# First cross-attention of a Perceiver stack: another order for the preparation of the keys

## Chip, cores and metric

The kernel runs on one core of one Trainium2 chip. The metric is the device time of one execution in microseconds (us). Before the change it was 652.71 us, the median of 3 runs (652.16 to 653.26). The core has five engines that run on their own and meet through semaphores: PE (TensorE: matmuls and, ahead of them, weight loads), DVE (VectorE), ACT (ScalarE), POOL (GpSimd) and SP (SyncE, which issues most of the DMAs). Each works through its own instructions in order.

## The reference

Twelve layers work one after the other on a latent array x of 2 batches by 64 rows by 256: four rounds of a cross-attention to a context (2 by 1024 rows by 192), a mixing layer and a mixture of experts. Only the first cross-attention is touched by the change:

```python
xn = layernorm(context)            # 2 x 1024 x 192
ln = layernorm(layernorm(x))       # 2 x 64 x 256
q = ln @ Wq.T
kv = concat([xn @ Wkv.T, ln @ Wlkv.T])       # 1024 context keys and 64 latent keys
q, k, v = split_heads(...)         # 4 heads of 64
qn, kn = rmsnorm(q) * qn_g / 8, rmsnorm(k) * kn_g
attn = softmax(where(mask, qn @ kn.T, -max)) # the latent keys are never masked
x = x + (attn @ v) @ Wo.T + bo
```

## The kernel before

The whole stack is one program. The first attention is the stage `l0x` (from L1148), about 9 to 78 us of the span. All 2 x 64 latent rows lie on the 128 partitions.

**Keys.** The context keys are made in four groups of 512, each one batch and two of its four key tiles in both halves; groups 0 and 1 are the first batch, 2 and 3 the second. A fifth group, LAT, is the latents' own keys and queries. For a group g these helpers are called, each of which emits instructions for one or two engines:

- `statistics(g)` (L1230): eight small DVE operations for mean and variance of four row tiles; `roots(g)` (L1238): the square root on ACT and its inverse on DVE; `normalise_rows(g)` (L1311): four POOL operations that normalise the context rows for use as values.
- `project(g)` (L1241): 16 matmul instructions into a pair of PSUM banks; `take(g)` (L1256): four DVE operations that scale the result by the inverse root and add a bias, into `kq`.
- `squares(g)` (L1265): one ACT operation; `sums(g)` (L1271): a DVE reduction and a square root on ACT; `over_rms(g)` (L1279): two small DVE operations and a large one that scales the keys.
- `turn_keys(g)` (L1288): for each half of the features four transposes on PE into one PSUM bank, and an ACT copy from it to `kT`. For LAT there are two transposes and three ACT copies for each half.

**Attention.** There are four query blocks a, b, c, d (batch and pair of heads). `scores(k)` (L1337) writes the scores of the context keys to a bank pair and those of the latent keys to a single bank, `extra`. `softmax(k)` (L1351) masks both with a custom DVE operation that also gives the minimum, and then takes the exponentials on ACT. `divisor`, `turn_p` (nine transposes into three single banks, emptied by DVE, ACT, DVE), `value_weights`, `weigh`, `turn_u` and `heads_of` follow. `hide_keys` (L1186) makes the mask on POOL.

**Fills.** `kv1.values_apart(b, t)` (L475) computes values of a later layer (`l1x`) in between. It is a generator: its first step takes two single banks and emits eight matmuls (half of the work), the second step the other eight, and the last two ACT copies that empty the banks. `steps(fill, 1)` runs one step, `steps(fill)` the rest. Another generator of the next stage, `kv1.keys` (L446, L451), is started right behind this stage with three steps.

**What sets the order.** The stage lies in `in_written_order()` (L295), which chains the instructions of PE, DVE, ACT and POOL each in the order in which the code emits them. So the code's order is the order on each engine, and an instruction that waits holds up all behind it on its engine. The three steps of `kv1.keys` lie outside and are placed by the framework's planner. PSUM is split into two pairs of banks and four single banks (`psum(2, 4)`); a bank is given to the next tile when the last reader of the old one is through. SBUF tiles rotate in the same way: `kq` and `p` (squares, then probabilities) have two buffers each.

The loop over the groups (L1452 to L1480) emits for g = 0 to 3: take and squares of the next group, over_rms of this one, the first half of a fill, turn_keys of this one (for g = 0 also LAT's and the fourth projection), sums of the next group, for g < 2 statistics, roots and row normalisation of group g + 2, then scores (a at g = 1, b at g = 2), at g = 2 also the table for the exponentials and the softmax of a, and the rest of the fill.

Of the kernel before, what the change touches and what calls it, by code (L numbers as in the profile page):

```python
# [12 lines left out]
AF = mybir.ActivationFunctionType  # L13
# [45 lines left out]
def tile_perceiver(ctx: ExitStack, tc: tile.TileContext, i: dict, out: bass.AP):  # L59
    nc = tc.nc  # L60
# [40 lines left out]
    def stat(n=1, name="stat"):  # L101
        return small.tile([P, n], F32, tag=f"s{n}", bufs=12 if n == 1 else 4, name=name)
# [130 lines left out]
    def table_for(func, behind):  # L233

        nc.scalar.activation(junk, behind, func, scale=0.0)  # L235

    def rstd_of(var, n=1, then=None, bias=eps, scale=1.0):

        root, r = stat(n, "root"), stat(n, "rstd")
        nc.scalar.activation(root, var, AF.Sqrt, bias=bias, scale=scale)  # L240
        if then is not None:
            table_for(then, root[:, 0:1])
        nc.vector.reciprocal(r, root)  # L243
        return r
# [288 lines left out]
    def steps(work, n=9):  # L533

        for _, _ in zip(range(n), work):
            pass
# [610 lines left out]
    with psum(2, 4), stage_pool(name="l0x", bufs=1) as pool, stage_pool(  # L1147
# [38 lines left out]
        def hide_keys():  # L1186
            nc.gpsimd.tensor_scalar(hide, m8, -1.0, BIG, ALU.add, ALU.mult)
# [42 lines left out]
        def statistics(g):  # L1230
            b, t = groups[g]
            mv[g] = small.tile([P, 4, 2], F32, tag="cx_mv", name="cx_mv")
            for k in range(4):
                st = stat(6, "bn_st")
                nc.vector.bn_stats(st, xh[:, b, k // 2, t + k % 2, :CD])
                nc.vector.bn_aggr(mv[g][:, k, :], st)

        def roots(g):  # L1238
            rstd[g] = rstd_of(mv[g][:, :, 1], 4)

        def project(g):  # L1241
            if g == LAT:
                kq[g] = prep.tile([P, 2, D], F32, tag="kql", bufs=1, name="kql")
                ps = bank()
                accumulate(ps, [(latT[:, c, :], wlkv[:, c, :]) for c in range(2)])
                return ps
            kq[g] = prep.tile([P, 4, D], F32, tag="kq", name="kq")
            ps = two_banks()
            context_values(ps, wkc, *groups[g])
            return ps  # L1250
# [6 lines left out]
        def take(g, ps):  # L1257
            for k in range(4):
                nc.vector.scalar_tensor_tensor(
                    kq[g][:, k, :], ps[:, k * D : (k + 1) * D], rstd[g][:, k : k + 1], bwk,  # L1260
                    ALU.mult, ALU.add,
                )
# [3 lines left out]
        def squares(g):  # L1266
            n = 2 if g == LAT else 4
            sq[g] = prep.tile([P, 4, D], F32, tag="p", name="sq")
            nc.scalar.activation(sq[g][:, :n], kq[g][:, :n], AF.Square)

        def sums(g):  # L1271
            n = 2 if g == LAT else 4
            rn[g] = stat(16, "rn")[:, : 4 * n]
            nc.vector.tensor_reduce(
                rn[g], sq[g][:, :n].rearrange("p t (h d) -> p (t h) d", h=4), AX.X, ALU.add
            )
            nc.scalar.activation(rn[g], rn[g], AF.Sqrt)

        def over_rms(g):  # L1279
            n = 2 if g == LAT else 4  # L1280
            nc.vector.tensor_scalar(rn[g], rn[g], 0.125, 1e-8, ALU.mult, ALU.max)
            nc.vector.reciprocal(rn[g], rn[g])
            by_head = kq[g][:, :n].rearrange("p t (h d) -> p (t h) d", h=4)
            nc.vector.tensor_tensor(
                by_head, by_head, rn[g].unsqueeze(2).to_broadcast([P, 4 * n, 64]), ALU.mult
            )

        def turn_keys(g):  # L1288
            n = 2 if g == LAT else 4
            for c in range(2):  # L1290
                ps = bank()
                for k in range(n):
                    nc.tensor.transpose(
                        ps[:, k * P : (k + 1) * P], kq[g][:, k, c * P : (c + 1) * P], ident
                    )
                if g == LAT:
                    nc.scalar.activation(kTl[:, c, :], ps[:, :P], AF.Copy, scale=col("l0x_kg"))
                    for h in range(2):
                        r = half[h]
                        nc.scalar.activation(  # L1300
                            qx[r, c, :, r],
                            ps[r, P : 2 * P].rearrange("p (b q) -> p b q", b=NB),
                            AF.Copy, scale=gq[r],
                        )
                else:
                    b, t = groups[g]
                    nc.scalar.activation(
                        kT[:, c, b, :, t : t + 2, :],
                        ps.rearrange("p (n t k) -> p n t k", n=2, t=2),
                        AF.Copy, scale=col("l0x_kg"),  # L1310
                    )  # L1311

        def normalise_rows(g):
            b, t = groups[g]
            for k in range(4):
                one = xh[:, b, k // 2, t + k % 2, :CD]
                nc.gpsimd.tensor_scalar(  # L1317
                    one, one, mv[g][:, k, 0:1], rstd[g][:, k : k + 1],
                    ALU.subtract, ALU.mult,
                )  # L1320
# [17 lines left out]
        def scores(k):  # L1338
            b, j = k
            q = qx[:, j, b, :]  # L1340
            sc[k], extra = two_banks(), bank()
            dst = [sc[k][:, n * 512 : (n + 1) * 512] for n in range(2)]
            for n in range(2):
                nc.tensor.matmul(
                    dst[n], q, kT[:, j, b, n].rearrange("p t k -> p (t k)"),
                    start=True, stop=True,
                )
            nc.tensor.matmul(extra[:, :P], q, kTl[:, j, :], start=True, stop=True)
            sc[k] = sc[k], extra

        def softmax(k):  # L1351

            main, extra = sc[k]
            b, _ = k
            neg, total = stat(2, "neg"), stat(2, "tot")
            p[k] = prep.tile([P, NK + P], F32, tag="p", name="p")
            for n, (keys, src, hidden_) in enumerate((
                (slice(NK, NK + P), extra[:, :P], hide_l[:, b, :]),
                (slice(0, NK), main, hide[:, b, :]),
            )):  # L1360
                nc.vector.tensor_tensor_reduce(
                    p[k][:, keys], src, hidden_, -1.0, NEG, ALU.add, ALU.min, neg[:, n : n + 1]
                )
            nc.vector.tensor_tensor(neg[:, 0:1], neg[:, 0:1], neg[:, 1:2], ALU.min)
            for n, keys in enumerate((slice(0, NK), slice(NK, NK + P))):
                nc.scalar.activation(
                    p[k][:, keys], p[k][:, keys], AF.Exp, bias=neg[:, 0:1], scale=-1.0,
                    accum_out=total[:, n : n + 1],
                )
            rinv[k] = total  # L1370
# [8 lines left out]
        def turn_p(k):  # L1379
            pT[k] = transposed(p[k], 9, prep, "pT", "pT")  # L1380
# [52 lines left out]
        psk = [project(0)]  # L1433
        statistics(0)
        roots(0)
        statistics(1)
        key_bias()
        psq = project_queries()
        roots(1)
        nc.scalar.copy(kq[LAT][:, 1, :], psq[:, :D])  # L1440
        take(0, psk[0])
        squares(LAT)
# [6 lines left out]
        normalise_rows(1)  # L1449
        psk.append(project(2))  # L1450
        a, b, c, d = ((b, j) for b in range(NB) for j in range(2))
        for g in range(4):  # L1452


            if g < 3:
                take(g + 1, psk[g + 1])
                squares(g + 1)
            over_rms(g)
            if g < 3:
                fill = kv1.values_apart(g // 2, 2 * (g % 2))  # L1460
                steps(fill, 1)
            turn_keys(g)
            if g == 0:
                turn_keys(LAT)
                psk.append(project(3))
            if g < 3:
                sums(g + 1)
            if g < 2:
                statistics(g + 2)
                roots(g + 2)  # L1470
                normalise_rows(g + 2)
            if g == 0:
                hide_keys()
            if g == 1:
                scores(a)
            if g == 2:
                scores(b)
                table_for(AF.Exp, rn[3][:, 0:1])
                softmax(a)
            if g < 3:  # L1480
                steps(fill)
        divisor(a)
        turn_p(a)
        softmax(b)
        value_weights()
        weigh(a)
# [1 line left out]
        divisor(b)  # L1488
        turn_p(b)
        turn_u(a)  # L1490
        softmax(c)
        weigh(b)
        scores(d)
# [1 line left out]
        divisor(c)  # L1495
        turn_p(c)
        turn_u(b)
        softmax(d)
        weigh(c)
        heads_of(b)  # L1500
# [1351 lines left out]
```

## Time and profile before

| what | value |
|---|---|
| median of the runs | 652.71 us |
| the profiled execution | 652.64 us |
| its span | 650.7 us |
| mean granted PE clock | 0.991 |
| first attention, statistics to its result | about 10.9 to 78.2 us |
| first scores (a) on PE | 35.01 us |
| first exponentials (a) on ACT | 45.83 us |
| value weights on PE | 50.11 us |
| result x of the stage on DVE | 77.81 us |

A row of the timeline gives the start in us from the span's start, the time that the instructions of one group took, the engine, the line, the operation, the tile written and the tiles read, the shapes and how many. Square brackets give how long the engine had been idle before it, and what ended the idle time. Matmuls are pipelined, so the time of several is less than the sum of their durations. A table by stretch gives for each engine the busy time and the number of instructions, and then the granted PE clock, the busy share of the DMA engines and GB/s.

### The profile page before, as it was taken

The page shows a single profiled execution, that of the slowest core. Times are in us where ns is not written, and L with a number is a line of the kernel's source. Part 1 is how long each engine was busy: PE and PEld are TensorE (multiplying, and loading weights), DVE is VectorE, ACT ScalarE, POOL GpSimd, SP SyncE. Part 2 cuts the span into 40 slices and gives each one's busy share as a digit, 9 for nine tenths or more (in the row PEclk, how much of TensorE's full clock was granted, in tenths as well). Part 3 has the DMA queues.
Part 4 walks back from the last instruction along what each step waited for, and adds up shares of the span by engine and source line. Part 5 has one row for each costly group of instructions (what it writes and reads, how often), then busy time and mean ns, then how long its engine had stood idle before and what let it go on. Part 6 is the DMA issues. An engine that isn't in the chain of part 4 may idle for free. (4 is left out here: it accounts for less than half of the span.)

```text
span 650.7 us, 11687 instructions
## 1 busy us (share of the span) xinstructions
PE 615.7 (95%) x4722; PEld 451.5 (69%) x4722; DVE 306.9 (47%) x871; ACT 258.4 (40%) x507; POOL 52.3 (8%) x88
## 2 busy tenths in 40 slices
PE   7989999999999969999999999999999989989996
PEld 3547659766754538999998688999984446775434
DVE  5875451268672014545554426625425247747111
ACT  2464462378732232323232434504422159742111
POOL 3540000000100000000000040040000000100000
PEclk9999999999999979999999999999999999999999
DMA  8970025920438477000000500010147910094870
GB/s 286 399 301 1 17 74 169 318 95 2 165 121 352 151 211 248 1 1 2 1 2 0 195 1 1 1 62 6 65 156 286 393 74 3 2 372 153 346 311 11
DMA packets 19441, 87.05 MB, mean 134 GB/s; under 512 B 2080, under 2 KB 6704, under 8 KB 11088
## 3 DMA queue, kind: packets, MB, share of 16 engines
q1 hardware_dynamic: 19120, 86.09, 35.8%
q8 instruction: 49, 0.80, 0.5%
q14 instruction: 16, 0.13, 0.1%
q10 hardware_dynamic: 256, 0.03, 0.0%
HBM read 85.98 MB, written 0.13 MB: 132 GB/s over the span
## 5 line engine op out<-in xcount | busy, mean ns | idle before, releaser
L2079 PE MATMUL bank<-l2x_ctx,p 128*128 128x193 f32 x256 | 48.1, 327 | 0.0
L2079 PEld LDWEIGHTS bank<-l2x_ctx,p 128*128 128x128 f32 x256 | 40.8, 190 | 0.4
L1714 DVE CUSTOM_DVE_ANT_0 p<-two_banks,zero 128x1024 f32<-128x1024 f32 x32 | 38.6, 1216 | 5.2 <-PE two_banks L1704 5.0
L1722 ACT ACTIVATE p<-p,negmax 128x1024 f32<-128x1024 f32 x32 | 36.9, 1154 | 4.7 <-DVE negmax L1714 4.7
L2043 DVE TENSOR_REDUCE l2x_mx<-two_banks 128x128 f32<-128x1024 f32 x16 | 19.6, 1225 | 26.5 <-PE two_banks L2035 26.5
L2028 PE MATMUL two_banks<-l2x_qA,ctxA 128*128 128x128 f32 x256 | 31.9, 278 | 0.0
L2028 PEld LDWEIGHTS two_banks<-l2x_qA,ctxA 128*128 128x128 f32 x256 | 30.3, 192 | 1.1 <-issue 1.0
L776 DVE COPY m_hT<-bank 128x512 f32<-128x512 f32 x12 | 8.3, 691 | 42.5 <-PE bank L770 42.5
L331 PE MATMUL bank<-ctxA,ones 128*128 128x256 f32 x94 | 25.8, 391 | 1.3 <-ACTq L1132 1.0
L2065 DVE TENSOR_TENSOR p<-two_banks,l2x_shift 128x512 f32<-128x512 f32 x32 | 20.6, 686 | 13.2 <-ACT l2x_shift L2060 13.2
L750 ACT ACTIVATE m_g<-two_banks 128x512 f32<-128x512 f32 x12 | 7.2, 598 | 47.1 <-PE two_banks L727 31.8
L235 ACT ACT_TABLE_LOAD x20 | 25.7, 1283 | 0.3
L751 DVE TENSOR_TENSOR m_prod<-two_banks,m_g 128x512 f32<-128x512 f32 x12 | 8.3, 691 | 35.8 <-ACT m_g L750 35.8
L2072 ACT ACTIVATE p<-p 128x512 f32<-128x512 f32 x32 | 19.7, 632 | 12.2 <-DVE p L2065 12.2
L1729 PEld LDWEIGHTS two_banks<-ident,p 128*128 128x128 f32 x128 | 13.7, 141 | 11.0 <-ACT pT L1758 9.1
L331 PEld LDWEIGHTS bank<-ctxA,ones 128*128 128x128 f32 x94 | 15.9, 190 | 5.6 <-issue 2.2
L1704 PE MATMUL two_banks<-n_kT,n_qx 32*128 32x512 f32 x128 | 19.2, 640 | 0.0
L1729 PE MATMUL bank<-ident,p 128*128 128x128 f32 x128 | 18.5, 280 | 0.5
L2035 PE MATMUL two_banks<-l2x_qB,ctxB 64*128 64x128 f32 x256 | 18.6, 285 | 0.0
L1317 POOL TENSOR_SCALAR xh<-xh,cx_mv,rstd 128x192 f32<-128x192 f32 x16 | 17.2, 1092 | 14.2 <-DVE rstd L243 14.2
L2099 ACT COPY l2x_uT<-bank 96x256 f32<-96x256 f32 x16 | 5.9, 370 | 30.8 <-PE bank L2096 30.8
L791 ACT COPY m_y<-bank 128x256 f32<-128x256 f32 x12 | 4.5, 373 | 33.9 <-PE bank L784 31.2
(658 smaller groups left out, 1349.3 us busy)
## 6 DMA issues: line engine op xcount, KB each, us to landing
l1f_w_sb<-in_l1f_w_dram SPq DMA_DIRECT2D x12, 1024.0 KB, 5.9
l3f_w_sb<-in_l3f_w_dram SPq DMA_DIRECT2D x12, 1024.0 KB, 8.2
more_w<-in_l3f_w_dram SPq DMA_DIRECT2D x12, 1024.0 KB, 9.0
l0f_w_sb<-in_l0f_w_dram SPq DMA_DIRECT2D x8, 1024.0 KB, 9.2
l2f_w_sb<-in_l2f_w_dram SPq DMA_DIRECT2D x8, 1024.0 KB, 4.9
more_w<-in_l1f_w_dram SPq DMA_DIRECT2D x4, 1024.0 KB, 6.1
more_w<-in_l2f_w_dram SPq DMA_DIRECT2D x6, 512.0 KB, 8.0
xh<-in_ctx_dram SPq DMA_DIRECT2D x8, 192.0 KB, 6.0
```

Source lines behind the costliest of these rows:

```text
L235: nc.scalar.activation(junk, behind, func, scale=0.0)
L331: nc.tensor.matmul(ps[:, :D], ones, ctxA[:, 0, 0, :D], start=True, stop=True)
L1704: nc.tensor.matmul(sc[u][:, n * 512 : (n + 1) * 512], qx[c, n][rows_, b].rearrange("p h q -> p (h q)"), kT[c, b][rows_, n, :], start=True, ...
L1714: nc.vector.tensor_tensor_reduce(p[u], sc[u], zero.to_broadcast([P, NK]), -1.0, 3.0e38, ALU.add, ALU.min, least)
L1722: nc.scalar.activation(p[u], p[u], AF.Exp, bias=sc[u], scale=-1.0, accum_out=total[u // 4][:, u % 4 : u % 4 + 1],)
L1729: nc.tensor.transpose(ps[:, kc * P : (kc + 1) * P], p[u][:, (4 * k + kc) * P : (4 * k + kc + 1) * P], ident,)
L2028: nc.tensor.matmul(sc[k][:, n, t, :], ctxA[:, b, n, t * P : (t + 1) * P], qA[:, j, b].rearrange("p h q -> p (h q)"), start=(t == 0), stop= ...
L2035: nc.tensor.matmul(sc[k][:, n, t, :], ctxB[half[n], b, t * P : (t + 1) * P], qB[half[n], j, b].rearrange("p h q -> p (h q)"), start=False, ...
L2043: nc.vector.tensor_reduce(mx[k], sc[k].rearrange("p n t q -> p q (n t)"), AX.X, ALU.max)
L2065: nc.vector.tensor_tensor(p[k][:, n], sc[k][:, n], shifts[k].unsqueeze(1).to_broadcast([P, 4, P]), ALU.add,)
L2072: nc.scalar.activation(p[k][:, n], p[k][:, n], AF.Exp)
L2079: nc.tensor.matmul(po[k][:, : CD + 1], p[k][:, kc // 4, kc % 4, :], crows[:, b * 8 + kc, :], start=(kc == 0), stop=(kc == 7),)
```

## The change

`roots` is split into `roots` (the square root on ACT) and `inverses` (DVE). `softmax` is split into `hidden` (the masking and the minimum on DVE) and `softmax` (the exponentials on ACT). The loop over the groups is written out, in another order:

- The root of the third group is issued ahead of LAT's copies on ACT.
- The squares of the next group stand on ACT ahead of the copies of a fill.
- The second fill's first half follows the second group's transposes, and its second half the third group's; the third fill lies around the last group's transposes.
- The third group is scaled (`over_rms(2)`) ahead of the fourth group's inverse and `take(3)`.
- The mask is made ahead of the third group's row normalisation on POOL.
- Block a is masked ahead of the fourth group's sums on DVE; block b behind `turn_p(a)`, as it was.

```diff
         def roots(g):
-            rstd[g] = rstd_of(mv[g][:, :, 1], 4)
+            rstd[g] = stat(4, "root")
+            nc.scalar.activation(rstd[g], mv[g][:, :, 1], AF.Sqrt, bias=eps, scale=1.0)
+
+        def inverses(g):
+            root, rstd[g] = rstd[g], stat(4, "rstd")
+            nc.vector.reciprocal(rstd[g], root)
...
-        def softmax(k):
+        def hidden(k):
...
             nc.vector.tensor_tensor(neg[:, 0:1], neg[:, 0:1], neg[:, 1:2], ALU.min)
+
+        def softmax(k):
+
+            neg, total = rinv[k], stat(2, "tot")
...
-        for g in range(4):
-
-
-            if g < 3:
-                take(g + 1, psk[g + 1])
-                squares(g + 1)
-            over_rms(g)
-            if g < 3:
-                fill = kv1.values_apart(g // 2, 2 * (g % 2))
-                steps(fill, 1)
-            turn_keys(g)
-            if g == 0:
-                turn_keys(LAT)
-                psk.append(project(3))
-            if g < 3:
-                sums(g + 1)
-            if g < 2:
-                statistics(g + 2)
-                roots(g + 2)
-                normalise_rows(g + 2)
-            if g == 0:
-                hide_keys()
-            if g == 1:
-                scores(a)
-            if g == 2:
-                scores(b)
-                table_for(AF.Exp, rn[3][:, 0:1])
-                softmax(a)
-            if g < 3:
-                steps(fill)
+        take(1, psk[1])
+        squares(1)
+        over_rms(0)
+        fill = kv1.values_apart(0, 0)
+        steps(fill, 1)
+        turn_keys(0)
+        sums(1)
+        statistics(2)
+        roots(2)
+        inverses(2)
+        turn_keys(LAT)
+        psk.append(project(3))
+        hide_keys()
+        normalise_rows(2)
+        take(2, psk[2])
+        squares(2)
+        steps(fill)
+        over_rms(1)
+        turn_keys(1)
+        sums(2)
+        statistics(3)
+        roots(3)
+        fill = kv1.values_apart(0, 2)
+        steps(fill, 1)
+        scores(a)
+        over_rms(2)
+        inverses(3)
+        normalise_rows(3)
+        turn_keys(2)
+        take(3, psk[3])
+        squares(3)
+        hidden(a)
+        sums(3)
+        steps(fill)
+        scores(b)
+        table_for(AF.Exp, rn[3][:, 0:1])
+        over_rms(3)
+        fill = kv1.values_apart(1, 0)
+        steps(fill, 1)
+        softmax(a)
+        turn_keys(3)
+        steps(fill)
         divisor(a)
         turn_p(a)
+        hidden(b)
         softmax(b)
```

`inverses(0)`, `inverses(1)`, `hidden(c)` and `hidden(d)` stand right behind or ahead of the call that they were split from.

## The prediction

> **What bounds the stage now.** I read the busy times by stretch of the span, then the order of time from 20 to 78 us, then each engine's waits. The page's first part says that TensorE (PE) is the bound: any time that it stands still in this first attention is time of the kernel, and any wait elsewhere counts only when PE ends up in it.
>
> ```profile
> PE 615.7 (95%) x4722; PEld 451.5 (69%) x4722; DVE 306.9 (47%) x871; ACT 258.4 (40%) x507; POOL 52.3 (8%) x88
> ```
>
> By stretch (PE first, then weight loads, DVE, ACT, POOL, granted clock):
>
> ```profile
> 31.00:41.00 10.00, 9.21 (x44) 4.99 (x42) 7.94 (x19) 5.74 (x10) 7.70 (x8) 1.00 1.01 418
> 41.00:51.00 10.00, 7.90 (x43) 4.87 (x43) 6.70 (x18) 7.30 (x14) 1.94 (x2) 1.00 0.35 135
> 51.00:64.00 13.00, 12.87 (x78) 10.16 (x78) 6.68 (x23) 5.03 (x13) 0.00 (x0) 1.00 0.01 1
> ```
>
> PE loses 0.8 and 2.1 us in the first two stretches and next to nothing from 51 us on. So the change is worth what it moves the moment at which PE turns to the value weights (50.11); behind that the order of every engine is as before. In order of time, the rows that decide it:
>
> ```profile
> 28.60 0.28 ACT L240 ACTIVATE root<-cx_mv,eps 128x4 f32<-128x4 f32 x1
> 28.92 0.18 DVE L243 RECIPROCAL rstd<-root 128x4 f32<-128x4 f32 x1 [1.61 <-ACT root L240]
> 33.96 1.22 DVE L1274 TENSOR_REDUCE rn<-sq 128x16 f32<-128x1024 f32 x1 [1.22 <-ACT sq L1269]
> 35.01 1.96 PE L1344 MATMUL two_banks<-kT,qx 128*128 128x512 f32 x4 [0.43 <-ACT kT L1307]
> 41.51 0.63 PE L1293 MATMUL bank<-ident,kq 128*128 128x128 f32 x4 [0.82 <-DVE kq L1284]
> 42.92 0.66 PE L1293 MATMUL bank<-ident,kq 128*128 128x128 f32 x4 [0.78 <-ACT kT L1307]
> 44.42 1.28 ACT L235 ACT_TABLE_LOAD   x1
> 45.83 1.14 ACT L1366 ACTIVATE p<-p,neg 128x1024 f32<-128x1024 f32 x1
> 47.35 1.05 ACT L531 COPY n_v<-bank 128x512 f32<-128x512 f32 x2
> 48.72 1.41 PE L272 MATMUL bank<-ident,p 128*128 128x128 f32 x9
> 50.11 1.02 PE L1326 MATMUL bank<-l0x_wv,ctx_gb 96*1 96x256 f32 x4
> 55.73 1.15 PE L272 MATMUL bank<-ident,p 128*128 128x128 f32 x9
> ```
>
> The reader is to see four things. DVE stands 1.61 us at 28.9 for the third group's root, which ACT issues behind six latent copies (26.43 to 28.45). At 42.92 the second transposes of a group wait for ACT to empty the bank of the first: of four single banks, two hold a fill and one the extra scores of a query block, which stay there until its masking has read them. At 45.83 ACT starts the first exponentials, behind a 1.28 us table load. And turning the first block's weights takes 1.41 us for nine transposes where the next block's nine take 1.15 (the row at 55.73): again banks, this time waiting for ACT's copies at 48.5 and 49.1. So from 42 us on PE is fed by ACT through four banks.
>
> **The change, step by step.** It adds no arithmetic and no DMA: the split of roots and of softmax emits the same instructions, so the sum is about places. "Pitch" is the distance from one start to the next in these rows.
>
> 1. *Roots ahead of the latent copies.* Statistics of the third group end at 27.31 (27.12+0.18). ACT is then free (the first group's key copies end at 26.5), so the root runs at 27.4 instead of 28.60, the inverse at 27.7, and take(2) starts at 28.0 instead of 29.20: DVE gains 1.2 us. The latent copies, 2.0 us, now run 27.6 to 29.6; only the first scores need them, at 34.4: free. If something needed them before 29.6, up to 1.2 us would come back.
> 2. *Squares ahead of the fill's copies.* squares(2) follows at 29.7 to 30.8, so the 1.22 us stall of the reduction at 33.96 goes: DVE runs take 1.57, small operations 0.5, scaling 1.40, reduction 1.13, statistics 1.87 without a stop, 28.0 to 34.5.
> 3. *Third group's scaling ahead of the fourth's projection.* It starts at 34.5 and ends at 34.5+0.20+0.29+1.23 = 36.2. PE, relieved of its wait at 35.01, has by 36.35 done what it had done by 37.03. Scaling to transpose costs 0.15 (47.68 to 47.82), so the third group's transposes start at 36.4: DVE and PE arrive together.
> 4. *Same bank wait.* As at 42.18 to 43.61, the second bank's copy starts 1.44 us after the first's: 37.0, then 38.45, ending 39.1. take(3) ends at 38.1 and the masking of block a (1.62 us) at 39.6, hidden while ACT is busy.
> 5. *ACT becomes a chain.* squares(3) 39.1 to 40.1; reduction on DVE to 41.35; root 41.4; the fill's two copies 41.5 to 42.5, which used to stand behind; table load to 43.8; exponentials at 43.9 instead of 45.83: 1.9 us gained.
> 6. *Where it goes.* PE has done scores b (1.94) and half a fill (1.69) from 39.9 and begins the last group's transposes at 43.5 (scaling done at 43.4). Now two banks hold the fill, which is only half written, and one the extra scores of b, whose masking has been put behind turn_p(a). One bank is left. Its copy stands on ACT behind the exponentials: 43.9+1.52 = 45.4 to 46.1. So PE stands from about 44.1 to 46.1, where before it had a second bank. Then 0.49 for four transposes, 1.69 for the second half of the fill to 48.3, its copies at 48.4 and 48.9, and the weights of a are turned as those banks come free: 48.3, 49.0, 49.5. The ninth transpose stood at 49.81 before.
>
> The sum is 49.5 - 49.8 = -0.3 us. Queues passed: on POOL the mask goes from 33.71 to 21.85, in a hole of 7.34 us; its source was issued at 12.02 and SP, which reuses the same landing semaphore eight issues later, passed at 17.88, so it is there. SP's queue is not touched. The row normalisations of groups three and four move by -1.2 us each and are used past 63 us.
>
> **Unknown: DVE beside POOL.** The mask (1.90 us, to 23.75) now runs beside the first group's scaling at 23.08. The rows that bear on it:
>
> ```profile
> 23.08 1.23 DVE L1284 TENSOR_TENSOR kq<-kq,rn 128x1024 f32<-128x1024 f32 x1
> 31.26 1.48 DVE L1284 TENSOR_TENSOR kq<-kq,rn 128x1024 f32<-128x1024 f32 x1
> 29.20 4.43 POOL L1317 TENSOR_SCALAR xh<-xh,cx_mv,rstd 128x192 f32<-128x192 f32 x4 [7.34 <-DVE rstd L243]
> ```
>
> Alone the scaling takes 1.23, beside POOL 1.48. Bounds: 0 (the mask's last third leaves it alone) and 0.67 (it waits for the mask's end). I take 0.25, the same operation beside POOL; PE absorbs little of it, +0.2 at the end. At 0.67 it is +0.6. With the -0.3 the sum is -0.1.
>
> The Trainium skill, page "SBUF — State Buffer", section "Who interferes with whom", states that the pair of ports which VectorE and GpSimd share is an exclusive lock and the loser blocks fully. By it the cost would be the 0.67 and the change +0.3; the row at 31.26 began 0.9 us before its POOL neighbour ended and lost only 0.25, so I go by the row.
>
> Summed in this same way, the rows of before give 49.4 for the ninth transpose that stands at 49.81: small waits for two semaphores are not in it. If the new chain has as many, that is +0.4. So the unknowns span -0.3 to +0.7 about the sum. The profiled execution took 652.64 us (span 650.7 and 1.9 around it); less 0.1 is 652.5, and the median lies 0.07 above that execution: **652.6 us**, own range 652.2 to 653.3.
>
> **Rivals.** A measurement of this kernel tells about 0.2% (1.3 us) from no change.
>
> *Faster, the bank wait of step 6 does not arise* (650.3). If block b's extra scores gave their bank back earlier, the last transposes end at 44.5, the fill at 46.2, and the turning of a is paced by ACT's four copies after 45.4, with the ninth at about 47.3: -2.4. Against it: the 1.41 us for nine at 48.72 is explained only if that bank is held.
>
> *Faster, key matmuls of the next stage move into the new hole* (650.9). Four (L446, L451) are outside the written order and are placed by a planner; now they stand at 63.70, 68.00, 73.61 and 75.02. Without them turn_u(b) would start 0.5 earlier, turn_p(d) 0.4, turn_u(d) 0.9: -1.8. Their PSUM pair is free from 39.6 to 53.6. Against it: it was free from 43.9 to 53.8 before, PE had a hole of 0.8 at 47.0, and it was not used.
>
> *Slower, masking a blocks beside POOL* (654.0). It now runs at 38.0 beside the fourth group's row normalisation (four operations of 1.0, to about 40.8), where at 42.42 POOL had one small addition. Its slack is 0.5 us; beyond that every us goes through the ACT chain. If each of its two passes waits for a POOL operation, 2.0, the price is 1.5. Against it: take(3), which also reads PSUM, took 1.66 for its four pieces at 37.82 beside POOL, and take(1) 1.65 at 21.03 with POOL idle for half of it.
>
> *Slower, the chain of steps 3 to 6 slips.* Some fourteen hand-offs follow each other; at 0.1 more each it is +1.4 (654.0); before, PE's waits hid some. It decides above 0.1 each.
>
> *Slower, the PE clock drops* in the 2 us hole (657). The only halving in the records runs from 235.5 to 245.8, after PE stood 5.52 us; here 10 us at half speed behind 46 us would cost 4 to 5. Against it: from 39.90 to 43.30 PE was busy 1.79 of 3.40 at full clock, and from 524.90 to 528.30 only 1.56; the new hole leaves about 1.5.
>
> The Trainium skill, page "TensorE: Matmul & The Clock Gate", section "HAM oscillation — how this bites in real kernels", sets the limit at idle gaps above about 3.4 us, which this hole does not reach.
>
> **How the numbers follow.** The forecast 0.49, no bank wait 0.10, key matmuls moved 0.12, another gain over 1.3 us (my chain too long) 0.06, masking blocked 0.06, chain slips 0.12, clock 0.05. Faster 0.28, same 0.49, slower 0.23. The range takes in the moved matmuls and the slip, 650.7 to 654.2, and leaves out the first rival and the clock.
>
> **What will show it.** Right: root of group three at 27.4, first exponentials near 44, the last group's second transposes waiting for ACT's copy until 46, the ninth transpose of a within 0.5 us of 49.8, and the same rows behind it. Wrong: no such wait; L446 ahead of 50 us; the masking of a longer than 2.2 us; the first scaling beyond 1.5; a clock below 1 between 44 and 60.

## The result, and the profile after

The changed kernel takes 655.46 us, the median of 7 runs (654.75 to 657.38), against 652.71 us before (7 runs): a ratio of 1.0043 with a 95% interval of 1.0028 to 1.0057. It is 2.75 us slower. The forecast was 652.6 us with a range up to 654.2 us, so it was wrong.

The busy times on the page of the kernel after:

```profile
PE 617.0 (94%) x4722; PEld 452.6 (69%) x4722; DVE 308.0 (47%) x871; ACT 258.1 (40%) x507; POOL 52.1 (8%) x88
```

Two stretches of the kernel after, the one in which the time goes and one behind it (columns: the stretch, its length, then busy time with the number of instructions for PE, weight loads, DVE, ACT and POOL, then the granted PE clock, the DMA share and GB/s):

```profile
41.00:51.00 10.00, 6.81 (x26) 4.07 (x25) 3.39 (x7) 5.57 (x12) 1.03 (x2) 0.83 0.36 137
54.00:67.00 13.00, 12.87 (x78) 10.16 (x78) 6.73 (x22) 4.95 (x13) 0.00 (x0) 1.00 0.01 1
```

From 41 to 51 us PE is busy 6.81 us instead of 7.90, and its clock, which was 1.00 there, is 0.83. The thirteen us behind the value weights look as they did before the change. The rows of the timeline after the change, in order of time:

```profile
21.86 1.90 POOL L1187 TENSOR_SCALAR hide<-m 128x2048 bf16<-128x2048 uint8 x1
22.52 1.27 DVE L1286 TENSOR_SCALAR rn<-rn 128x16 f32<-128x16 f32 x1
35.24 1.98 PE L1349 MATMUL two_banks<-kT,qx 128*128 128x512 f32 x4
43.49 1.28 ACT L235 ACT_TABLE_LOAD   x1
44.90 1.13 ACT L1375 ACTIVATE p<-p,neg 128x1024 f32<-128x1024 f32 x1
45.02 0.18 DVE L1286 TENSOR_SCALAR rn<-rn 128x16 f32<-128x16 f32 x1 [2.76 <-ACT junk L235]
45.52 1.22 DVE L1289 TENSOR_TENSOR kq<-kq,rn 128x1024 f32<-128x1024 f32 x1
46.89 0.63 PE L1298 MATMUL bank<-ident,kq 128*128 128x128 f32 x4 [2.42 <-DVE rinv L1384]
47.55 0.69 ACT L1312 ACTIVATE kT<-bank,cols 128x512 f32<-128x512 f32 x1 [1.05 <-PE bank L1298]
48.29 1.11 PE L1298 MATMUL bank<-ident,kq 128*128 128x128 f32 x4 [0.78 <-ACT kT L1312]
49.20 1.91 PE L482 MATMUL bank<-l1x_wv_sb,ctxA 128*128 128x256 f32 x4
51.68 1.56 PE L272 MATMUL bank<-ident,p 128*128 128x128 f32 x9
53.17 1.02 PE L1331 MATMUL bank<-l0x_wv,ctx_gb 96*1 96x256 f32 x4
```

Three things differ from the forecast. At 22.52 the first small operation of the first group's scaling takes 1.27 us where it took 0.16: it ends 0.03 us after POOL's mask. At 45.02 the last group's scaling has waited 2.76 us for `junk`, the dummy operation that brings in the exponentials' table, so PE stands for 2.42 us before the last transposes. (The bracket there names `rinv`, but the transposes read `kq`, whose scaling runs from 45.52 to 46.74.) And from 48.29 the matmuls are slow: four of the fill take 1.91 us where such a row shows 1.03 elsewhere.

The value weights come at 53.17 instead of 50.11. The start of the stage moves from execution to execution: `take(1)`, which takes the second group's projection, starts between 20.95 and 22.27 us in the profiles of this study. It follows the PE clock: the first clock record, at full speed, begins at 10.1 us in the profile with `take(1)` at 20.95 and at 12.3 us in the one with 22.27 (the table by another tile), and the other profiles lie between in nearly the same order. The landing of the context does not explain it: the first statistics start at 10.85 us in the kernel before, with `take(1)` at 21.03, and already at 10.17 in the profile with the latest `take(1)`. The first four projection matmuls of these two profiles:

```profile
10.65 1.03 PE L421 MATMUL two_banks<-wkc,ctxA 128*128 128x256 f32 x4
11.01 1.69 PE L421 MATMUL two_banks<-wkc,ctxA 128*128 128x256 f32 x4
```

So the profiles are compared by times from the start of `take(1)`. There the value weights stand at 29.07 before and 32.22 after, 3.15 us later. From them to the result x it is 27.70 or 27.71 us in every profile of this study, so nothing of the difference arises between the two. Behind x the rest of the program takes 571.2 to 573.4 us; it is shortest in the three profiles in which PE runs at half clock near 236 us for 6.83 us and not for 10.24.

In the table the ratios are to the runs of the kernel before that were made together with each kernel (medians 652.51 to 652.87).

| kernel | large scaling of group 4 | exponentials a | last transposes, first and second bank | value weights | median, us | ratio to before (95%) |
|---|---|---|---|---|---|---|
| before | 25.42 | 24.80 | 26.79, 27.25 | 29.07 | 652.71 | 1 |
| after | 24.57 | 23.95 | 25.94, 27.34 | 32.22 | 655.46 | 1.0043 (1.0028 to 1.0057) |
| after, mask late | 23.45 | 22.83 | 24.82, 26.23 | 31.21 | 654.6 | 1.0026 (1.0008 to 1.0045) |
| after, table by another tile | 20.97 | 22.82 | 22.34, 25.06 | 28.63 | 653.49 | 1.0007 (0.9995 to 1.0019) |
| after, both | 21.00 | 22.86 | 22.37, 25.09 | 28.66 | 652.65 | 0.9989 (0.9976 to 1.0003) |
| after, PE kept busy | 23.44 | 22.82 | 24.82, 26.22 | 29.79 | 653.36 | 1.0012 (0.9998 to 1.0026) |
| after, b masked early | 23.64 | 23.01 | 25.01, 25.47 | 28.72 | 653.22 | 1.0006 (0.9989 to 1.0023) |
| after, mask late, other tile, b early | 20.98 | 22.84 | 22.36, 22.84 | 26.51 | 650.38 | 0.9957 (0.9942 to 0.9973) |
| before, table by another tile | 23.79 | 24.68 | 25.80, 26.81 | 28.73 | 652.52 | 1.0003 (0.999 to 1.0015) |
| before, mask early | 25.48 | 24.85 | 26.85, 27.31 | 29.13 | 653.28 | 1.0008 (0.9994 to 1.0023) |
| after, mask late, PE busy | 23.44 | 22.82 | 24.81, 26.22 | 29.79 | 653.18 | 0.9998 (0.9974 to 1.0022) |
| after, second profile | 23.57 | 22.95 | 24.94, 26.35 | 31.45 | 655.24, one run | |
| after, mask late, second profile | 23.44 | 22.82 | 24.81, 26.22 | 29.79 | 654.04, one run | |

### The profile page after: what moved, and what is told of

The parts are those of the page before. It is cut to its first block, busy times and chain, and to the rows that moved or that the text cites. A ratio compares the mean times of both kernels' runs of the same rounds, so it can differ in the third digit from the quotient of the medians.

```text
span 653.2 us, 11685 instructions
## 1 busy us (share of the span) xinstructions
PE 617.0 (94%) x4722; PEld 452.6 (69%) x4722; DVE 308.0 (47%) x871; ACT 258.1 (40%) x507; POOL 52.1 (8%) x88
## 5 line engine op out<-in xcount | busy, mean ns | idle before, releaser
L2098 ACT ACTIVATE p<-p 128x512 f32<-128x512 f32 x32 | 19.6, 630 | 12.2 <-DVE p L2091 12.2
```

Source lines behind the costliest of these rows:

```text
L2098: nc.scalar.activation(p[k][:, n], p[k][:, n], AF.Exp)
```

## The experiments

**The mask late.**

```diff
-        hide_keys()
         normalise_rows(2)
+        hide_keys()
```

> The changed kernel with the mask on POOL behind the third group's row normalisation again. Theory A: the +3.06 us at the value weights (50.11 to 53.17) are +1.0 from the mask blocking DVE's first small scaling operation (1.27 us at 22.52 instead of 0.16), +1.1 from the last group's scaling, which waits for the table load's dummy operation because that reads the same tile rn[3] (DVE idle 2.76 us before 45.02), +1.2 from PE at half clock from 47.7 to 51.1, and -0.3 as forecast. It expects here: the small operation at 0.16, exponentials of a at 43.9 (44.90 with the mask early), value weights at 52.2, time 1.0 us below the changed kernel. Rival B: the ACT chain with its four banks alone sets the end and takes up an earlier loss; it expects the value weights within 0.3 us of 53.2.

The small operation takes 0.16 us again and the exponentials come 1.12 us earlier, counted from take(1), 22.83 against 23.95; the value weights come 1.01 us earlier. Nothing on the way takes the loss up, so rival B falls. The median falls by 0.9 us, but its runs spread from 651.89 to 657.11; more on that below.

**The table by another tile.** `table_for` reads one column of a tile only to have something to read. In the changed kernel, as before, it is `rn[3]`, which `over_rms(3)` then overwrites in place; the write has to wait for the read, and the read for the table load.

```diff
-        table_for(AF.Exp, rn[3][:, 0:1])
+        table_for(AF.Exp, rn[2][:, 0:1])
```

> The changed kernel, but the dummy operation that brings in the exponentials' table reads the third group's roots (rn[2], done long before) instead of the fourth's. Theory A: the last group's scaling no longer waits for it: its first small operation at 42.6 instead of 45.02, first transposes of the last group near 44.5, their copy at 46.4 behind the exponentials instead of 47.55, so value weights 1.1 us earlier, 52.0 (50.9 if the clock stays full as well). Rival C: the wait before 45.02 is for the root on ACT and not for the dummy; nothing moves.

The timeline of DVE in this kernel:

```profile
42.74 0.17 DVE L1286 TENSOR_SCALAR rn<-rn 128x16 f32<-128x16 f32 x1 [0.28 <-ACT rn L1282]
43.24 1.22 DVE L1289 TENSOR_TENSOR kq<-kq,rn 128x1024 f32<-128x1024 f32 x1
```

The wait is 0.28 us and for the root, as it should be. Theory A holds and rival C falls. This profile had a late start in which the mask ended (23.16) before the small operation began (23.83), so it shows no mask cost. Nor did its clock drop: behind a hole of 2.07 us instead of 2.41 us the value weights stand at 28.63. What the table's wait alone costs is the difference to the next kernel but one, where the wait is there and the clock is full: 29.79 - 28.63 = 1.16 us.

**Both.**

> Both edits together, mask late and table by another tile. Theory A: the two losses lie one behind the other, so both come back: value weights 2.1 us earlier than in the changed kernel, at 51.1 with the half clock still there, at 49.9 without it; the time between 0.2 us below and 1 us above the kernel before. Rival B: no more than the larger of the two, about 52.0.

The timeline of this kernel in the stretch that the forecast's sixth step speaks of:

```profile
41.89 0.17 DVE L1286 TENSOR_SCALAR rn<-rn 128x16 f32<-128x16 f32 x1 [0.28 <-ACT rn L1282]
43.76 0.65 PE L1298 MATMUL bank<-ident,kq 128*128 128x128 f32 x4
45.76 0.67 ACT L1312 ACTIVATE kT<-bank,cols 128x512 f32<-128x512 f32 x1
46.48 0.66 PE L1298 MATMUL bank<-ident,kq 128*128 128x128 f32 x4 [2.07 <-ACT kT L1312]
50.04 1.02 PE L1331 MATMUL bank<-l0x_wv,ctx_gb 96*1 96x256 f32 x4
```

This is the forecast's picture: transposes at once, one bank left, 2.07 us of PE waiting for the copy behind the exponentials. The value weights stand at 28.66, 0.41 us before those of the kernel before; the forecast without its mask term was -0.3. The time is the same as before within the interval. More came back than theory A had listed (3.56 us instead of 2.1 in the profile), because the clock stayed full as well.

**PE kept busy.** Five extra matmuls, whose result nobody reads, ahead of the last transposes; no wait is removed.

```diff
         softmax(a)
+        keep_busy(5, two_banks())
         turn_keys(3)
```

> The changed kernel with five extra dummy matmuls (128x256, into a bank pair that is free then, never read) on PE ahead of the last group's transposes, where PE stands for 2.41 us. No wait is taken away. Theory A: they fit in the hole (five times 0.43), the clock stays full from 44 to 60, the last group's second transposes and the rest of the fill take 2.2 us instead of 3.4, value weights 1.2 us earlier, 52.0, time 1.2 us below the changed kernel. Rival D: the slow stretch from 48.3 to 51.1 is something else than the clock, a bank or an issue wait; then it stays, and the dummies cost 0 to 0.5 us.

PE in this kernel:

```profile
44.55 2.43 PE L331 MATMUL two_banks<-ctxA,ones 128*128 128x256 f32 x10
47.04 0.63 PE L1298 MATMUL bank<-ident,kq 128*128 128x128 f32 x4
48.44 0.66 PE L1298 MATMUL bank<-ident,kq 128*128 128x128 f32 x4 [0.78 <-ACT kT L1312]
48.94 1.03 PE L482 MATMUL bank<-l1x_wv_sb,ctxA 128*128 128x256 f32 x4
```

The fill's matmuls are back at 1.03 us, and the records show no half clock between 12.2 and 237.5 us. The first row is the dummies, two instructions each. Value weights at 29.79 with the same last transposes as in the kernel with the mask late (31.21): the slow stretch costs 1.42 us there. Theory A holds, rival D falls. Not all of the 2.1 us by which the median falls below that of the changed kernel comes from this stage: five of the twelve executions had a mean clock of 0.994, and in the profiled one of them the half clock near 236 us lasted 6.83 us instead of 10.24.

**Block b masked early.** `hidden(b)` moves from behind `turn_p(a)` to behind `over_rms(3)`.

```diff
         over_rms(3)
+        hidden(b)
         fill = kv1.values_apart(1, 0)
...
         turn_p(a)
-        hidden(b)
         softmax(b)
```

> The changed kernel, but block b is masked on DVE right behind the last group's scaling instead of behind turn_p(a), so that the bank of its extra scores comes free about 4 us sooner. Counted from the start of take(1), the value weights stand at 29.07 before the change and 32.22 after it. Theory A (one bank was left, and the last group's second transposes waited for a copy behind the exponentials): the second transposes follow the first without the wait of 1.05 us; turning the weights of a no longer waits for the fill's copies; the hole of 2.41 us ahead of the first transposes stays, and with it perhaps the half clock; value weights at 28.4 plus 1.1 (mask) plus 1.3 (clock), so 28.4 to 30.8. Rival B: the wait is for ACT and not for a bank; the second transposes still start about 1.4 us behind the first.

The timeline of PE in this kernel:

```profile
46.02 1.06 PE L1298 MATMUL bank<-ident,kq 128*128 128x128 f32 x8 [2.41 <-DVE kq L1289]
46.92 1.03 PE L482 MATMUL bank<-l1x_wv_sb,ctxA 128*128 128x256 f32 x4
48.51 1.20 PE L272 MATMUL bank<-ident,p 128*128 128x128 f32 x9
```

On PE all eight transposes now run in one go, and nine transposes of a take 1.20 us instead of 1.56. So it was the bank held for b, and rival B falls. The value weights stand at 28.72 with the hole of 2.41 us and, in this profile, a full clock. Six of the twelve executions had a mean clock of 0.989 or less and took 653.98 to 654.87 us, the other six 649.66 to 652.45.

**All three repairs.**

> The changed order with three repairs: mask on POOL late, table by another tile, block b masked behind the last group's scaling. Theory A: no hole of 2 us is left on PE; last transposes at 22.4 and 22.8 from take(1), the fill's second half to 25.0, the ninth transpose of a when ACT has copied two groups and a half fill behind the exponentials, 26.2; value weights at 26.5 against 29.07 before, time 2.5 us below the kernel before. Rival E: something behind the value weights (exponentials of b, the copies of pT) takes most of it back; the result x of the stage then comes less than 1.2 us earlier than 56.78.

The timeline of this kernel over the same stretch, DVE's masking of b and then PE:

```profile
43.87 0.28 DVE L1366 CUSTOM_DVE_ANT_0 p<-bank,hide_l 128x128 f32<-128x128 f32 x1
44.10 1.08 PE L1298 MATMUL bank<-ident,kq 128*128 128x128 f32 x8
45.02 1.03 PE L482 MATMUL bank<-l1x_wv_sb,ctxA 128*128 128x256 f32 x4
46.82 1.38 PE L272 MATMUL bank<-ident,p 128*128 128x128 f32 x9
48.26 1.02 PE L1331 MATMUL bank<-l0x_wv,ctx_gb 96*1 96x256 f32 x4
```

The masking frees the bank 0.4 us before the second transposes want it; PE no longer stands. Value weights at 26.51, where 26.5 was expected, and all of it reaches the result x, 54.22 us from take(1) instead of 56.78; rival E falls. The median is 650.38 us, 0.43% below the kernel before (0.27% to 0.58%). Part of this is again the clock near 236 us: four of the nine executions had a mean clock of 0.994, and three of the 32 of the kernel before had as much or more. The five at 0.991 have a median of 650.94 us, against 652.67 for the 24 of the kernel before at this clock, which is 1.7 us less; the highest of the five, 651.03, lies below the lowest of the 24, 651.15. So this version beats both.

**The same two edits on the kernel before.**

> The kernel before, with only the table's dummy operation reading another tile. There too DVE waits 1.92 us for it. Theory A: the last scaling starts 1.5 us earlier, PE begins the last transposes 0.8 us earlier, but ACT copies them only behind the exponentials and the fill as before, so value weights within 0.3 us of 29.07 from take(1), time the same. Rival F: this wait costs the kernel before as much as the changed one, and the time falls by about 0.8 to 1.2 us.

> The kernel before, with only the mask on POOL moved ahead of the third group's row normalisation. Theory A: where POOL reaches it while DVE starts the first group's scaling, the small operation there takes up to 1.3 us instead of 0.16 and all behind it comes up to 1.1 us later, value weights at 29.1 to 30.2 from take(1); the median rises by 0 to 1 us, because the landing of the context moves POOL against DVE from run to run. Rival G: the block is taken up by the waits that the kernel before has at 28.9 and 33.9, and nothing changes behind 35 us.

The other tile moves the value weights by 0.34 us (29.07 to 28.73), a little more than the 0.3 allowed, and the time not measurably. Before the change DVE waited for the dummy as well (1.92 us), but PE was behind anyhow, and ACT copied the last group only behind the fill. The early mask on the kernel before cost 0.17 us at the small operation (0.33 us long) in its profile and 0.06 us at the value weights; the median is 0.4 us higher, with an interval that includes nothing at all. How much the mask costs depends on when POOL and DVE come to it (DVE's side follows the clock, as told above, and not the landing that the expectation names): in the profile of the changed kernel it ran from 21.86 to 23.76 beside an operation that was due at 22.52, in others from 21.0 to 22.9 or so, and one that was due at 23.8 met nothing. In the second profile of the changed kernel the two rows are:

```profile
21.08 1.90 POOL L1187 TENSOR_SCALAR hide<-m 128x2048 bf16<-128x2048 uint8 x1
22.73 0.28 DVE L1286 TENSOR_SCALAR rn<-rn 128x16 f32<-128x16 f32 x1
```

In all four profiles in which the two met, the small operation ended 0.03 us after the mask (at 23.79, 23.01, 22.93 and 22.89 us). So its price there is what is left of the mask when it is due. What it adds to the median of the changed kernel is between 0 and 1.1 us; the times do not settle it.

**The clock, once more.**

> The changed kernel with the mask late and with the five dummy matmuls in PE's hole. So far: with the mask late alone, six of twelve executions had a mean granted clock of 0.989 or less and took 655.4 to 657.1 us, the six at 0.991 or more 651.9 to 653.8. Theory A: the hole is what makes the clock drop; with it filled no execution falls below 0.990, the upper group vanishes, median 653.2, value weights at 29.8 from take(1) (31.2 with the hole). Rival H: the two groups come from elsewhere in the program (the half-clock stretch near 236 us is in every kernel); then a group at 0.989 or less remains.

> The changed kernel once more, for a second profile. Theory A: the hole of 2.4 us ahead of the last group's transposes and the wait for the dummy operation are there again; the mask's cost lies between 0 and 1.1 us by when POOL reaches it; half clock again within 2 us of the hole's end, for 3.4 us or more. Rival: the half clock of the first profile was a single event and does not come back.

> The changed kernel with the mask late once more, for a second profile: the hole is the same 2.41 us; whether the clock drops behind it varies from execution to execution (half of twelve so far). With a drop value weights at 31.2 or later from take(1), without one at 29.8.

The second profile of the changed kernel has the hole (2.42 us), the half clock from 47.88 to 51.30 and the value weights at 31.45, with a mask cost of 0.13 us. The second profile of the kernel with the mask late has the same hole of 2.41 us and no half clock in this stage, with the value weights at 29.79. So one program gives 31.21 and 29.79, and the difference is the clock. The stretch behind the hole in the kernel with the mask late, in its first profile:

```profile
48.70:52.10 3.40, 3.40 (x13) 2.07 (x12) 0.10 (x1) 1.53 (x3) 0.00 (x0) 0.50 0.00 0
```

A stretch of the same length from the start of the last group's second transposes in its second profile:

```profile
48.30:51.70 3.40, 3.32 (x21) 2.29 (x21) 0.66 (x1) 1.77 (x3) 0.00 (x0) 1.00 0.00 0
```

In 3.40 us there are 13 matmul instructions at clock 0.50 and 21 at 1.00. Of the twelve timed executions of this kernel six had a mean clock of 0.989 or less and took 655.39 to 657.11 us, six had 0.991 or more and took 651.89 to 653.81. All seven of the changed kernel were at 0.989 or less. With the hole filled and the mask late one of twelve was below 0.990 (0.986, 658.89 us), where none was expected, and four more took 654.46 to 655.01 us at 0.991; with the hole filled and the mask early one of twelve was below (0.988, 655.49 us). So the upper group is nearly but not quite gone, and these executions are not explained. A mean clock does not say where in the program the clock was halved: four of the six upper executions with the mask late had 0.986 or 0.987, less than the 0.989 of the profiled one.

The clock records of the profiles say more than the means. In all 13 profiles every stretch between two changes of the clock lasts a whole number of times 3.413 us: once at half clock in this stage, twice or three times near 236 us. So the changes lie on a grid that begins with the first full clock. These are the lengths of this grid at whose end the three drops of this stage came (the changed kernel, its second profile, the mask late), and then, in three profiles without a drop, the length around the hole with PE least busy (the second profile with the mask late, b masked early, both):

```profile
44.27:47.68 3.41, 0.83 (x6) 0.42 (x4) 2.17 (x6) 2.35 (x7) 0.00 (x0) 1.00 0.10 37
44.47:47.88 3.41, 1.00 (x7) 0.79 (x8) 1.98 (x5) 1.94 (x5) 0.00 (x0) 1.00 0.03 13
45.27:48.68 3.41, 1.54 (x10) 1.30 (x11) 1.47 (x4) 1.61 (x6) 0.00 (x0) 1.00 0.00 1
46.03:49.44 3.41, 1.80 (x12) 1.49 (x12) 1.21 (x4) 1.62 (x5) 0.00 (x0) 1.00 0.00 0
44.45:47.86 3.41, 1.84 (x12) 1.50 (x12) 3.27 (x10) 2.36 (x6) 0.00 (x0) 1.00 0.02 7
45.03:48.44 3.41, 1.96 (x12) 1.37 (x12) 0.61 (x3) 2.08 (x6) 0.00 (x0) 1.00 0.01 2
```

From the first full clock to 640 us, each such length at full clock with PE busy for 1.54 us or less was followed by half clock (16 of them, 13 ahead of the stretch near 236 us), and none with 1.80 us or more was. So one program drops or does not drop by where its hole falls on the grid, and the grid begins at another time in each execution. That this also sorts the timed executions, of which only the mean clock is kept, is not shown; nor is why the drop came in every execution of the changed kernel and in half of those that differ in the mask alone.

## Why the prediction was wrong

- **Steps 1 to 5 were right.** Where the mask does not interfere, the exponentials start at 22.82 to 22.86 from take(1); the forecast's 43.9 is 22.87.
- **Step 6 failed in its first sentence.** It put the last group's transposes at 43.5 because the scaling would be done at 43.4. They came at 46.89. The scaling overwrites the tile that the dummy operation reads, and now stood in front of everything else; the wait was in the profile before the change, as 1.92 us of DVE waiting for `junk`, and the forecast did not read it. It costs 1.16 us (1.13 us between the two profiles at full clock that have the mask late and differ in the tile alone). With another tile the transposes come at 22.37 from take(1), or 43.4, the copy behind the exponentials at 45.4, and the value weights 0.41 us before those of before. The bank wait that step 6 named is real: the early masking of b removes it.
- **The mask's price was taken at the wrong instruction.** The forecast priced the large scaling at 23.08, between 0 and 0.67 us, and took 0.25 from a row. What collided was the small operation 0.48 us ahead of it, which ended with the mask: 1.27 us instead of 0.16, and 1.11 us at the large scaling. So the range was too short by the head start of the small operation. In all four profiles in which the two met, the rule of the Trainium skill, page "SBUF — State Buffer", section "Who interferes with whom" (the loser blocks fully), fits better than the row chosen against it: the small operation ended 0.03 us after the mask. In three of the four only the mask's last 0.1 to 0.2 us was left.
- **The clock rival had its chance at 0.05 and came.** The forecast saw a hole of 2.0 us and took a full clock from two stretches with PE busy 1.56 and 1.79 of 3.40 us. These lie across the lengths of the grid; in the lengths themselves, where the clock of the kernel before stayed full, PE was busy for 2.13 us or more. The halving from 235.5 us was not the only one on record either: the clock fell again at 648.6, 2.8 us after PE's last matmul. The hole became 2.41 us, with only four transposes and another wait of 0.78 us behind it, and the clock was halved for 3.41 us. Its price was 1.3 to 1.5 us in the profiles, not 4 to 5, because it lasted a third as long as the one in the records of before. The limit of about 3.4 us that the Trainium skill, page "TensorE: Matmul & The Clock Gate", section "HAM oscillation — how this bites in real kernels", gives for idle gaps is not borne out: a hole of 2.41 us, with PE busy for 0.83 to 1.54 of the grid's 3.41 us, was enough here.
- **The other rivals did not come.** The masking of a took 1.63 us beside POOL (38.90 to 40.53), as it had alone; the key matmuls of the next stage stayed behind the value weights, at 66.77 to 78.09 us, each 3.07 to 3.08 us later than before; the chain did not slip.

The sum, from take(1) to the value weights in the profiled execution, goes along pairs of profiles that differ in one thing: -0.41 for the order itself (both repairs against before), +1.13 for the tile that the table's dummy reads, +1.42 for the clock (the two profiles with the mask late) and +1.01 for the mask (the changed kernel against the mask late). That is the 3.15 us measured, as each step starts where the last one ends. Taken elsewhere the terms differ a little: 1.16 for the tile, 1.11 for the mask at the large scaling, and an estimate of 1.3 to 1.5 for the clock in the two profiles of the changed kernel. One slip in the forecast decides nothing: the -0.3 to +0.7 us that it sets about its sum are, by its own terms, about no change.

## What to carry to other kernels

A reordering that moves an instruction forward makes every dependency of it count that was covered before, write after read on a scratch tile included; go through all the waits of the moved instruction in the profile, also those that cost nothing there. A hole of PE can cost more than its length: here one of 2.41 us cost another 1.4 us wherever it left PE busy for 1.54 us or less in one length of the clock's grid, and a few matmuls that nobody reads were cheaper than the clock that is lost. When a reordering ends where it began, look for the buffer that is still held: here masking b earlier, on top of the two other repairs, brought the value weights from 28.66 to 26.51 us and turned a draw into a gain of 0.3 to 0.4%.

## What the runs showed of the hardware

- The PE clock was halved for 3.41 us within 0.8 to 2.3 us of the end of a hole of 2.41 us, in some executions of one program and not in others. Behind holes of 2.07 us the two profiles show no halving, and two of 23 timed executions had a mean clock of 0.988 or 0.989.
- In 13 profiles the clock changed only on a grid of 3.413 us that began with the first full clock. It fell behind each length with PE busy for 1.54 us or less, and behind none with 1.80 us or more.
- A small DVE operation of 0.16 us on 128x16 values took 0.28 to 1.27 us beside a POOL operation and ended 0.03 us after it in all four profiles in which they met.
- The moment at which the clock first became full, between 10.1 and 12.3 us, moved this stage by up to 1.3 us between profiles of nearly the same program, which is half of the effect that was to be measured.
